# Layer 3's taps moved between TensorE and VectorE, and the next chunk's convolution and dt blocks paced over the scan steps

## The chip, the cores and the metric

The kernel runs on one core of one Trainium2 chip. The time is device time in microseconds of one launch. The engines are called as in the profile: PE is TensorE's matmul (PEld its weight load), DVE is VectorE, ACT is ScalarE, POOL is GpSimd, SP is SyncE, which here only issues DMAs.

## The reference, cut to what matters

Four residual layers on x of shape (8, 384, 32, 32), each after a group norm. Layers 0 and 2 hold a Mamba block over the 1024 positions of an image, layer 2 with a layer norm ahead and an MLP (384 to 1536 to 384) behind it. Layer 1 is a gated convolution with an 8x8 patch filter, layer 3 a depthwise 3x3 convolution.

```python
x = x + L0(_gn(x))      # Mamba
x = x + L1(_gn(x))      # 1x1, patch filter, depthwise 3x3, gate, 1x1
x = x + L2(_gn(x))      # layer norm, Mamba, MLP
x = x + L3(_gn(x))      # depthwise 3x3

# Mamba, per position l, channel d of 768, state n of 16
xm, z = split(x @ in_proj.T)
u  = silu(causal_conv3(xm) + conv_b)
dt, Bm, Cm = split(u @ x_proj.T)               # 24, 16, 16
dt = softplus(dt @ dt_proj.T + dt_b)
h  = exp(dt * A) * h + (dt * u) * Bm           # the scan over l
y  = (h . Cm + u * D) * silu(z)
out = y @ out_proj.T

# layer 3
conv_general_dilated(x, k, padding=1, feature_group_count=384)   # k: (384, 1, 3, 3)
```

## The kernel before, in words

**Tiling.** Each Mamba layer takes the 8 images as 16 chunks of T = 512 positions (two an image; chunk numbers n run from 0 to 15 for layer 0 and from 16 to 31 for layer 2, so that even n is an image's first half and odd n its second). The 768 x 16 states of a chunk are spread over 24 scan steps: a step holds 4 tiles of 128 partitions x 512 positions (8 channels x 16 states each). Steps are numbered through, 768 in all; `s["t"]` is the number of a chunk's first step (24 n). Six blocks of 128 channels (d = 0 to 5) make a chunk, and steps 4d to 4d+3 scan block d.

**One scan step** is made by nine generators (lines 745 to 900): `begins` loads g, the broadcast of dt*u, from DRAM up to five steps ahead (SP); `times` multiplies it by B (POOL, 128x2048); `decays` spreads dt by four matmuls into four PSUM tiles dA (PE); `exps` takes the exponent (ACT); `scans` runs four scans and two products with C (DVE); `states` does the other two products (POOL, 128x1024); `carries` saves the last column (ACT); `gathers` sums over states by matmuls into y (PE); `gatings` applies z (DVE).

**Work beside the scan.** While chunk n is scanned, the kernel prepares chunk n+1 and finishes earlier ones:
- `front` (line 594) of the next chunk: group norm (and layer norm), then six convolution blocks `block(d)` (line 619: three matmuls from in_proj, one ACT scale, two DVE multiply-adds; the function starts once chunk n-2's u buffers are free), SiLU, x_proj, and six dt blocks `step(d)` (line 668: one matmul, three ACT functions for softplus, a DVE add, the split of dt into three bf16 parts, one DMA `dtd`, and `scaled(d, v)`, line 718: dt*u on POOL and four DMAs `dud`). In layer 0 the split's first remainder is made by PE and the second by DVE; in layer 2 both are made by POOL.
- `gates` (line 548): the z projections and their SiLU. `finish` (line 905): the out-projection, which frees u, and in layer 2 the MLP (`mlp`, line 1152), one chunk after another.
- `layer1` (line 1020) and `layer3` (line 1215), once an image.

**Layer 3.** For each of three channel blocks k and two halves hf, `depthwise` (line 993) makes a diagonal 128x128 weight for each of the first `taps` taps (ACT) and multiplies it into one PSUM bank (PE); `take` (line 1242) then adds the other 9 - taps taps one after another by `scalar_tensor_tensor` on DVE, in the same bank, adds x and sends the result off. `TAPS, LAST_TAPS = 6, 4` (line 50): six taps on PE for images 0 to 6, four for image 7, whose layer 3 comes after the last scan. Layer 3 of image b runs for the most part from the middle of the next image's second chunk on.

**What sets the order.** `Order` (line 194 on) writes the program when the kernel is built: every piece of work is a generator that yields the engine it wants next and what must be ready; a clock model (`Clocks`) guesses when each engine is free, and of all that could begin, the earliest goes first. Each engine then runs its instructions in that fixed order and waits on semaphores. Nothing of the planner runs on the chip. Two helpers bear on the change:

```python
def pace(t):
    return once(lambda: ahead["scans"] >= 4 * min(t, len(steps)))
```

`pace(t)` holds a generator back until the planner has issued the scans of all steps before t; `together(due, gens)` starts several generators and waits for all. Three PSUM banks (`NBANK`) serve all products but dA and y; at most two dt blocks are between their matmul and their split at a time (`m_free`, `dt_free`, `pc_free`).

Of the kernel before, what the change touches and what calls it, by code (L numbers as in the profile page):

```python
# [17 lines left out]
B, C, H, W = 8, 384, 32, 32  # L18
# [8 lines left out]
NCH = L // T  # L27
# [19 lines left out]
NBANK = 3  # L47
LEAD = 2
PATIENCE = 6.0
TAPS, LAST_TAPS = 6, 4  # L50
SHARE = (2, 2, 2, 2)
SET_EXP = "natural_log_exp_and_others"

# [1 line left out]
def _flat(ap):  # L55
    return ap.rearrange("p a b -> p (a b)")


def _rows(ap):

    return ap.rearrange("(p k) l -> p k l", k=KC)
# [188 lines left out]
def tile_conv_preact_d4(ctx: ExitStack, tc: tile.TileContext, a: dict, out: bass.AP):  # L250
# [41 lines left out]
    def pace(t):  # L292

        return once(lambda: ahead["scans"] >= 4 * min(t, len(steps)))

    def once(test):
        return None, lambda: 0.0 if test() else None, None, False
# [38 lines left out]
    def product(name, pairs, when=None, read=()):  # L336

        ps = None
        for place, lhsT, rhs, start, stop in pairs:
            if ps is None:  # L340
                yield on("PE", rhs, lhsT, *read, when=both(bank, when) if when else bank)
                ps, tag = ps_take(name)
            else:
                yield on("PE", rhs, lhsT, next_=True)
            mm(place(ps), lhsT, rhs, start=start, stop=stop)
        return ps, tag
# [4 lines left out]
    def chain(name, terms, when=None, place=whole):  # L351
        terms = list(terms)
        last = len(terms) - 1
        return product(
            name,
            [(place, l, r, n == 0, n == last) for n, (l, r) in enumerate(terms)],
            when,
        )
# [172 lines left out]
    def projection(s, name, at):  # L531
        return chain(
            name, ((s["w"]["in"][:, k, at : at + P], s["xn"][:, k, :]) for k in range(KC))
        )
# [59 lines left out]
    def front(s):  # L594
        c, n, due = s["c"], s["n"], s["t"] - 26
        yield once(lambda: n == 0 or "normed" in chunks[n - 1] and (n == 1 or ("gates", 1) in chunks[n - 2]))
        yield on("SP")
        if n < NCH:
            xn = s["xn"] = first[n]
        else:  # L600
            xn = s["xn"] = new(wk, [P, KC, T], F32, "xf", 2)
            sync.dma_start(xn, _rows(s["src"][s["b"], :, c * T : (c + 1) * T]))
        if n % (B * NCH) == 0:
            yield from load_mamba(s["pre"])
        w = s["w"] = layer_w[s["pre"]]
        vec = w["vec"]
        yield once(lambda: "stats" in chunks[n - c])
        yield on("ACT", xn, chunks[n - c]["stats"][1])
        group_norm(_flat(xn), _flat(xn), chunks[n - c]["stats"])
        if s["pre"] == "l2_":  # L610
            yield from layer_norm(xn, due)
        s["normed"] = True
        yield once(lambda: n < 2 or "free" in chunks[n - 2])
        uh = s["u"] = [new(wk, [P, NH, T], F32, "u", 4) for _ in range(2)]
        u = [uh[d // NH][:, d % NH, :] for d in range(ND)]
        if c < NCH - 1:
            s["xt"] = new(wk, [P, ND, 2], F32, "xt")

        def block(d):
            ps, tag = yield from projection(s, "ps_in", d * P)  # L620
            yield on("ACT", ps)
            act(u[d], ps, AF.Identity, scale=vec[:, d, 2:3], bias=vec[:, d, 3:4])
            if c < NCH - 1:
                act(s["xt"][:, d, :], ps[:, T - 2 : T], AF.Copy)
            for j in (1, 2):
                yield on("DVE", u[d])
                vector.scalar_tensor_tensor(
                    u[d][:, j:T], ps[:, 0 : T - j], vec[:, d, 2 - j : 3 - j],
                    u[d][:, j:T], ALU.mult, ALU.add,
                )  # L630
            ps_give(ps, tag)

        yield from together(due, [block(d) for d in range(ND)])
        if c > 0:
            yield on("POOL", *u, due=-1)
            prev = chunks[n - 1]["xt"]
            hal = new(wk, [P, ND, 3], F32, "hal")
            gpsimd.tensor_mul(
                hal[:, :, 0:2], prev, vec[:, :, 0:1].to_broadcast([P, ND, 2])
            )  # L640
            gpsimd.tensor_mul(hal[:, :, 2:3], prev[:, :, 1:2], vec[:, :, 1:2])
            gpsimd.tensor_add(hal[:, :, 0:1], hal[:, :, 0:1], hal[:, :, 2:3])
            for h in range(2):
                gpsimd.tensor_add(
                    uh[h][:, :, 0:2], uh[h][:, :, 0:2], hal[:, h * NH : (h + 1) * NH, 0:2]
                )
        yield on("ACT", *u, when=session())
        for h in range(2):
            act(_flat(uh[h]), _flat(uh[h]), AF.Silu)
        exp_set()  # L650
        ps, tag = yield from chain(
            "ps_x", ((w["x"][:, d, :], u[d]) for d in range(ND)), place=lambda ps: ps[:RX, :]
        )
        yield once(lambda: n == 0 or "fronted" in chunks[n - 1])
        yield on("ACT", ps)
        dbc = new(wk, [RX, T], F32, "dbc")
        act(dbc, ps[:RX, :], AF.Identity, bias=one_row)
        ps_give(ps, tag)
        bc = s["bc"] = new(wk, [P, 2, T], F32, "bc", 2)
        s["dtd"], s["dud"], s["dts"] = {}, {}, {}  # L660

        def spread(j):
            ps, tag = yield from chain("ps_bc", [(selbc[:, j * P : (j + 1) * P], dbc)])
            yield on("ACT", ps)
            act(bc[:, j, :], ps, AF.Copy)
            ps_give(ps, tag)

        def step(d):
            ps, tag = yield from chain(
                "ps_dt", [(w["dt"][:, d * P : (d + 1) * P], dbc)],  # L670
                when=m_free.when,
            )
            m_free.take()
            m = new(wk, [P, T], F32, "spm", 2)
            yield on("ACT", ps)
            act(m, ps, AF.Abs)
            yield on("ACT", m)
            act(m, m, AF.Exp, scale=-1.0)
            yield on("ACT", m)
            act(m, m, AF.Ln, bias=1.0)  # L680
            yield on("DVE", m, when=dt_free.when)
            dt_free.take()
            v = new(wk, [P, T], F32, "dt", 2)
            vector.scalar_tensor_tensor(v, ps, 0.0, m, ALU.max, ALU.add)
            ps_give(ps, tag)
            yield on("ACT", v, when=pc_free.when)
            pc_free.take()
            pc = new(wk, [P, NPC, T], BF16, "pc", 2)
            act(pc[:, 0, :], v, AF.Copy)
            if s["pre"] == "l0_":  # L690
                yield on("PE", pc[:, 0, :], when=bank)
                rest, tag = ps_take("ps_dr")
                mm(rest, eye, v, stop=False)
                mm(rest, minus, pc[:, 0, :], start=False)
                m_free.give()
            else:
                yield on("POOL", pc[:, 0, :])
                gpsimd.tensor_sub(m, v, pc[:, 0, :])
                rest, tag = m, None
            order.add(scaled(d, v), s["t"] - 14)  # L700
            yield on("ACT", rest)
            act(pc[:, 1, :], rest, AF.Copy)
            if tag:
                yield on("DVE", pc[:, 1, :])
                vector.tensor_sub(pc[:, 2, :], rest, pc[:, 1, :])
                ps_give(rest, tag)
            else:
                yield on("POOL", pc[:, 1, :])
                gpsimd.tensor_sub(pc[:, 2, :], rest, pc[:, 1, :])
                m_free.give()  # L710
            yield on("SP", pc)
            to = dram.tile([NPC, P, T], BF16, tag="dtd", name="dtd", bufs=2 * ND)
            sync.dma_start(to.rearrange("p c t -> c p t"), pc)
            s["dtd"][d] = to
            pc_free.give()
            yield once(lambda: d in s["dud"])

        def scaled(d, v):
            yield on("POOL", u[d])
            gpsimd.tensor_mul(v, v, u[d])  # L720
            yield on("SP", v)
            to = dram.tile([E8 * NSUB, 4, T], F32, tag="dud", name="dud", bufs=2 * ND)
            for j in range(4):
                sync.dma_start(to[:, j, :], v[32 * j : 32 * (j + 1), :])
            s["dud"][d] = to
            dt_free.give()

        yield from together(due, [spread(j) for j in range(2)])
        yield from together(s["t"] - 14, [step(d) for d in range(ND)])
        s["fronted"] = True  # L730

# [733 lines left out]
```

## Time and profile before

| what | value |
|---|---|
| median of three runs | 6377.04 us (6371.48 to 6378.63) |
| the profiled execution | 6382.54 us, span 6380.8 us |
| first scan, last scan's end | 78.4 us, 6214.0 us |
| granted PE clock, mean | 0.964 |
| POOL, a step's two multiplies (128x2048, 128x1024) | 4537 ns + 2361 ns |
| DVE, a scan | 1205 to 1270 ns |
| DVE, a product with C | 675 ns |
| PE, matmul records of layer 3's depthwise | 552 |
| DVE, tap operations of layer 3 | 156 |

Busy time counts an engine's instructions as one union; the groups give the mean of one instruction and the idle time of its engine just before it, with what ended that. All engine calls go through one helper, so that all groups have its line, L189, and are told apart by their tiles. Tile names: `dA` decays, `g` the scanned input and result, `ps_in` convolution, `ps_dt`, `dt`, `spm`, `pc` the dt blocks, `ps_dw` from `xp` layer 3's depthwise (from `tp`: layer 1's), `ps_up`, `ps_dn`, `h` the MLP, `ps_out` the out-projection. A float32 matmul leaves two records.

### The profile page before, as it was taken

The numbers are of one execution on the slowest core, as the hardware profiler recorded it, in microseconds if no ns is written. First come the engines' busy times: TensorE is split into PE (matmuls) and PEld (weight loads), VectorE is DVE, ScalarE is ACT, GpSimd is POOL, SyncE is SP. The second block draws the span as 40 slices with busy tenths as digits, with TensorE's granted clock in tenths as the row PEclk, the third lists the DMA queues.
The fourth block names the chain that finished last, engine by engine and source line by source line (L and its number), as shares of the span: only waits on it lengthen the run. The fifth ranks groups of instructions, "written<-read, shape, count | busy, mean of one in ns | idle before, by whom it ended". The sixth has DMA issues, their size and how long they took to land.

```text
span 6380.8 us, 63205 instructions
## 1 busy us (share of the span) xinstructions
PE 5905.2 (93%) x19178; PEld 2228.3 (35%) x19178; DVE 5566.3 (87%) x6308; ACT 4268.3 (67%) x8024; POOL 5721.1 (90%) x2022
## 2 busy tenths in 40 slices
PE   6788999999999999989899999999999999999997
PEld 2223333333333333333333333333333333333333
DVE  4999989999999989988897898898988979989792
ACT  5666676767776666667766777667766667667652
POOL 4999999999999999989997998999989989989880
PEclk8789999999999999999999999999999999999998
DMA  6878778888877888877777787888778878878671
GB/s 167 196 190 199 176 192 191 200 198 210 188 188 189 190 190 189 199 187 185 181 181 194 196 207 184 192 209 200 197 178 196 204 185 197 186 197 202 173 177 37
DMA packets 345864, 1195.92 MB, mean 187 GB/s; under 512 B 40420, under 2 KB 142484, under 8 KB 247220
## 3 DMA queue, kind: packets, MB, share of 16 engines
q1 hardware_dynamic: 345524, 1191.88, 77.1%
q8 instruction: 154, 2.52, 0.2%
q14 instruction: 186, 1.52, 0.1%
HBM read 1040.73 MB, written 150.99 MB: 187 GB/s over the span
## 4 chain that ended last, share of the span: by engine, by line
DVE 30%; PE 27%; POOL 18%; ACT 10%; issue 9%; DMA 5%; SPq 0%; POOLq 0%; DVEq 0%; ACTq 0%
POOL g L189 17%; DVE g L189 14%; DVE dA L189 10%; PE ps_dw L189 5%; PE y L189 4%; DMA g<-dud 4%; PE ps_dn L189 3%; PE dA L189 3%; DVE u L189 3%; PE ps_up L189 3%; ACT dA L189 2%; PE ps_z L189 2%; PE ps_in L189 1%; ACT L370 1%; PE ps_t L189 1%
## 5 line engine op out<-in xcount | busy, mean ns | idle before, releaser
L189 POOL TENSOR_TENSOR g<-g,bc 128x1024 f32<-128x1024 f32 (+1 forms) x1536 | 5238.0, 3449 | 322.9 <-ACT carry L189 151.5
L189 ACT ACTIVATE dA<-dA,w_A 128x512 f32<-128x512 f32 x3072 | 2018.4, 661 | 1056.9 <-PE dA L189 1045.1
L189 PE MATMUL dA<-dts,selr 96*128 96x512 bf16 x3072 | 1192.9, 391 | 226.5 <-DVE g L189 207.5
L189 DVE TENSOR_TENSOR_SCAN g<-dA,carry,g 128x512 f32<-128x512 f32 x768 | 950.9, 1267 | 123.5 <-POOL g L189 108.0
L189 DVE TENSOR_TENSOR g<-dA,bc 128x512 f32<-128x512 f32 x1536 | 992.0, 675 | 24.3 <-ACT carry L189 23.3
L189 DVE TENSOR_TENSOR_SCAN g<-dA,g 128x512 f32<-128x512 f32 x768 | 903.3, 1205 | 111.2 <-POOL g L189 93.5
L189 DVE TENSOR_TENSOR_SCAN dA<-dA,carry,g 128x512 f32<-128x512 f32 x768 | 951.7, 1270 | 36.8 <-ACT dA L189 36.5
L189 DVE TENSOR_TENSOR_SCAN dA<-dA,g 128x512 f32<-128x512 f32 x768 | 907.0, 1210 | 62.6 <-ACT dA L189 62.4
L189 PE MATMUL y<-g,sely 128*32 128x512 f32 x6144 | 863.9, 631 | 64.8 <-POOL g L189 59.6
L189 PEld LDWEIGHTS <-selr 96*128 96x128 bf16 x3072 | 300.7, 99 | 1109.5 <-issue 1072.9
L189 PE MATMUL ps_dn<-h,mw 128*128 128x512 f32 x1152 | 563.4, 610 | 23.3 <-ACT h L189 11.8
L189 PE MATMUL ps_z<-xf,w_in 128*128 128x512 f32 x1152 | 567.5, 603 | 12.9 <-ACT z L189 5.2
L189 PE MATMUL ps_in<-xf,w_in 128*128 128x512 f32 x1152 | 551.1, 599 | 7.7 <-ACT xf L189 5.5
L189 PE MATMUL ps_up<-t,mw 128*128 128x512 f32 x1152 | 550.2, 596 | 7.1 <-ACT h L189 3.8
L189 PE MATMUL ps_out<-u,w_out 128*128 128x512 f32 x1152 | 551.6, 595 | 0.0
L189 PE MATMUL ps_dw<-tp,diag 128*128 128x512 f32 x864 | 436.5, 611 | 5.5 <-ACT diag L189 5.0
L189 PEld LDWEIGHTS y<-g,sely 128*32 128x32 f32 x6144 | 127.4, 109 | 628.5 <-POOL g L189 310.5
L189 PEld LDWEIGHTS ps_dn<-h,mw 128*128 128x128 f32 x1152 | 221.7, 196 | 290.5 <-issue 242.3
L189 PEld LDWEIGHTS ps_z<-xf,w_in 128*128 128x128 f32 x1152 | 218.0, 192 | 269.2 <-issue 213.7
L189 PEld LDWEIGHTS ps_in<-xf,w_in 128*128 128x128 f32 x1152 | 215.3, 191 | 275.5 <-issue 244.3
L189 PEld LDWEIGHTS ps_up<-t,mw 128*128 128x128 f32 x1152 | 214.6, 190 | 263.5 <-issue 228.2
L189 POOL TENSOR_TENSOR dt<-dt,u 128x512 f32<-128x512 f32 x192 | 243.2, 1277 | 70.5 <-ACT pc L189 61.3
(112 smaller groups left out, 6545.4 us busy)
## 6 DMA issues: line engine op xcount, KB each, us to landing
g<-dud SPq DMA_DIRECT2D x768, 1024.0 KB, 7.7
dtd<-pc SPq DMA_DIRECT2D x192, 384.0 KB, 4.0
dts<-dtd SPq DMA_DIRECT2D x192, 384.0 KB, 8.2
mw<-in_l_mlp_w SPq DMA_DIRECT2D x192, 384.0 KB, 6.4
dud<-dt SPq DMA_DIRECT2D x768, 64.0 KB, 3.0
xf<-in_x SPq DMA_DIRECT2D x16, 768.0 KB, 9.3
x<-in_x SPq DMA_DIRECT2D x16, 768.0 KB, 13.4
x_mid<-x SPq DMA_DIRECT2D x16, 768.0 KB, 5.1
```

What stands on the lines that cost most here:

```text
L189: return call(out_, *args, **kw)
L370: nc.scalar.preload_act_table_set(SET_EXP)
```

## The change

`TAPS` goes from 6 to 4, so that images 0 to 6 take four taps of layer 3 on PE and five on DVE, as image 7 did. In `front`, the convolution block d is not issued before step `s["t"] - 18 + d`, and the dt block d not before step `s["t"] - 9 + 3 * d`. Chunks 0, 15 and 16 are left as they were. Operations and buffers are otherwise the same.

```diff
-TAPS, LAST_TAPS = 6, 4
+TAPS, LAST_TAPS = 4, 4
...
         def block(d):
+            if n not in (0, B * NCH - 1, B * NCH):
+                yield pace(s["t"] - 18 + d)
             ps, tag = yield from projection(s, "ps_in", d * P)
             yield on("ACT", ps)
             act(u[d], ps, AF.Identity, scale=vec[:, d, 2:3], bias=vec[:, d, 3:4])
...
         def step(d):
+            if n not in (0, B * NCH - 1, B * NCH):
+                yield pace(s["t"] - 9 + 3 * d)
             ps, tag = yield from chain(
                 "ps_dt", [(w["dt"][:, d * P : (d + 1) * P], dbc)],
                 when=m_free.when,
```

## The prediction

> **What bounds the kernel now.** I read the page first (busy shares), then the groups by shape, then busy time by stretch, then the waits of the worst stretch.
>
> ```profile
> span 6380.8 us, 63205 instructions
> PE 5905.2 (93%) x19178; PEld 2228.3 (35%) x19178; DVE 5566.3 (87%) x6308; ACT 4268.3 (67%) x8024; POOL 5721.1 (90%) x2022
> ```
>
> Three engines are near full at once and ACT is not. An average does not say which one binds where, so I cut the trace at the start of each scan step (four DVE scans; 24 steps a chunk). First scan at 78 us, last scan's end at 6214 us. Chunks 2 to 14 (layer 0) take 179 us on average, chunks 18 to 29 (layer 2, with the MLP and layer 3 of earlier chunks) 201 us, and 167 us of tail follow. One image period of layer 2, from the answer for five stretches (columns: stretch, length, then busy us of PE, PEld, DVE, ACT, POOL; granted clock, DMA share, GB/s):
>
> ```profile
> 4931.62:5000.48 68.86, 60.32 (x179) 21.69 (x178) 64.08 (x76) 53.82 (x96) 64.06 (x32) 0.93 0.78 197
> 5000.48:5077.90 77.42, 75.97 (x247) 29.32 (x246) 70.36 (x80) 44.39 (x92) 67.15 (x20) 1.00 0.87 214
> 5077.90:5170.39 92.49, 89.53 (x302) 32.96 (x300) 88.45 (x100) 60.62 (x121) 92.33 (x33) 1.00 0.77 181
> 5170.39:5263.72 93.33, 88.80 (x252) 35.96 (x252) 53.13 (x59) 62.72 (x99) 65.31 (x33) 0.96 0.74 190
> 5263.72:5346.85 83.13, 81.80 (x272) 30.99 (x270) 81.55 (x92) 57.78 (x94) 78.65 (x24) 1.00 0.76 178
> ```
>
> These are **S1** odd chunk, steps 16 to 24 (five of the six layer-3 depthwise blocks start here); **S2** even chunk, steps 0 to 9; **S3** even, 9 to 22; **S4** even step 22 to odd step 5; **S5** odd, 5 to 16. Means of six such periods: S1 67.4 us (PE 62.0, DVE 63.6, POOL 65.1), S2 75.6 (73.7, 67.7, 66.3), S3 94.4 (91.6, 90.3, 93.9), S4 83.2 (78.8, 52.3, 63.9), S5 84.2 (82.6, 81.7, 80.3). S3 is POOL's (99%), S5 everybody's, S2 PE's. S4 is the loose one: seven steps in 83 us where seven at S3's pace (94.4/13) take 51, DVE idle for a third while PE is 95% busy. What it waits for:
>
> ```profile
> POOL spm L189 <- ACT pc L189: 19.3, 2, 10.0
> DVE x L189 <- PE ps_dn L189: 12.3, 3, 5.7
> DVE dt L189 <- ACT spm L189: 12.0, 2, 9.3
> DVE g L189 <- POOL g L189: 5.0, 2, 2.9
> ```
>
> The scans of the new odd chunk wait for its dt blocks, and those for a late front: its convolution starts 5 to 9 steps before the chunk in odd chunks (12 to 15 before even ones), because PE still has the MLP of older chunks to run.
>
> The groups that the change touches (busy us, mean ns, idle before):
>
> ```profile
> L189 PE MATMUL ps_dw<-xp,diag 128*128 128x512 f32 x552 | 280.1, 625 | 19.0 <-ACT diag L189 16.8 <-DVE dt L189 1.5 <-DVE acc L189 0.4
> L189 DVE SCALAR_TENSOR_TENSOR ps_dw<-xp,vec,ps_dw 128x512 f32<-128x512 f32 x156 | 115.2, 740 | 42.0 <-PE ps_dw L189 40.8
> L189 ACT ACTIVATE diag<-eye,vec 128x128 f32<-128x128 f32 x276 | 103.0, 405 | 47.7 <-PE ps_dw L189 46.8
> L189 POOL TENSOR_TENSOR dt<-dt,u 128x512 f32<-128x512 f32 x192 | 243.2, 1277 | 70.5 <-ACT pc L189 61.3
> L189 POOL TENSOR_TENSOR spm<-dt,pc 128x512 f32<-128x512 f32 x96 | 110.9, 1164 | 77.0 <-ACT pc L189 73.4 <-DMA g<-dud 3.4
> L189 POOL TENSOR_TENSOR pc<-spm,pc 128x512 bf16<-128x512 f32 x96 | 111.1, 1164 | 15.4 <-ACT pc L189 15.0
> ```
>
> A matmul's recorded duration is not its price, since records overlap:
>
> ```profile
> 4772.02 5.31 PE L189 MATMUL ps_z<-xf,w_in 128*128 128x512 f32 x12
> ```
>
> Twelve records in 5.31 us with a last one of 0.59 are 0.429 us apart. A float32 matmul has two records: **0.86 us each**.
>
> [...] I therefore price PE by starts. At 0.429 us a record a layer-2 chunk needs about 185 us, PE over 90% by that measure too. [...] the trace has 215 for the bf16 ones and twice that a record for float32. [...] The added DVE operation reads one tensor from PSUM and one from SBUF, and the 156 like it take 740 ns beside a POOL at 90%[...].
>
> **The change, part by part.**
>
> *Taps.* Images 0 to 6, six blocks each, two taps: 84. PE loses 84 x 0.86 = 72 us (10.3 an image). Upper end: the block's records start 0.50 us apart on average, waits for diagonals included, so up to 84 us. ACT loses 84 x 0.405 = 34 us: worth nothing where ACT is 64 to 79% busy (S1 to S5). DVE gains 84 x 0.74 = 62 us (8.9 an image). Image 7 already has four taps.
>
> *Convolution pacing* (block d not before step -18+d). Before, even layer-0 chunks start at -18 to -15, odd ones at -18 to -14, layer-2 chunks at -15 to -6. The pace holds back mostly even layer-0 chunks, by up to three steps, and their dt blocks then still begin near -9. I take 0: cover is the five or so steps until dt; were that gone, a boundary stall as in S4 would follow.
>
> *dt pacing* (block d not before step -9+3d: -9, -6, -3, 0, 3, 6). Before, six blocks come within some six steps ending near -2, in odd layer-2 chunks at -3 to +1. Block d is first used at step 4d, its load goes out up to five steps earlier: 4 to 5 steps of slack, no new stall. So blocks 3 to 5 move into the next chunk's steps 0 to 6. Each brings, in layer 2, POOL 1.28+1.16+1.16 = 3.6 us, PE 0.86, DVE 0.68, ACT about 3.1; in layer 0 POOL 1.28, DVE 1.35, PE 4 x 0.429 + 0.215 = 1.93; and on SP one dtd and four dud issues, about 2.1 us, in front of g loads that have four steps to spare.
>
> *Added waits.* The pace orders the program; no engine waits on it. The five chained DVE operations (3.7 us, were 2.2) hold a PSUM bank longer, while PE holds it 1.7 us less. Bounds -1 to +2 us an image; I take 0.
>
> *Layer 0* (means of six). Even 0 to 12: 101.9 us, PE 95.7; gets 5.8 of PE, I take half, +2.9. Even 12 to 24: 85.3, POOL 81.3; loses 3 x 1.28: -3.8. Odd 0 to 7: 49.4, PE 48.2; 5.8 less its 1.2 idle: +4.6. Odd 15 to 24: 64.3, POOL 64.3: -3.8. Sum -0.1 a pair: **0**, bounds +-4 on 6.5 pairs, +-26.
>
> *Layer 2, per image.* S1+S2 (143.0 us): DVE 131.3 + 8.9 = 140.2; at the 97% that DVE reaches in S5 that needs 144.5, at its present idle 11.7 it needs 151.9: +1.5 to +8.9, I take +2.5. POOL stays 131.4 over the two (10.8 moves from S1 to S2), PE falls by 10.3, which lets the MLP matmuls queued there go ahead. S3: POOL-bound, 0. S4: PE is 10.3 lighter before it, so MLP and out-projection end sooner, convolution and dt come sooner, and three dt blocks no longer crowd block 0; floor is POOL 63.9 + idle. I take -10 of a possible -19. S5: gets block 5, +1. Sum **-6.5**, six images: -39. Image 6 has its depthwise in chunk 31, where the last-but-one MLP runs until 6249 us, beyond the scans: -9 in the tail. Together **-48**. The profiled execution took 6382.5 (span 6380.8); -48 there is 6334, and from the median 6377.0 it is **6329**.
>
> **Rivals.**
> - *Larger gain, 6279.* S4 falls further towards its POOL floor: -14 an image, seven times, -98. For: S4's DVE is 31 of 83 us idle. Against: PE is 95% busy there and only 10 of that goes away.
> - *No change, 6377.* POOL binds S1, S3 and S5 (95 to 99%), and S4's gain is eaten by S1+S2. For: POOL's work is only moved.
> - *Slower, 6422: DVE becomes the bound in S1+S2.* Steps there stretch by the full 8.9 us an image (+62), the out-projection that frees the buffers of the odd chunk's convolution comes later with them, and S4 gives only the 2.4 from fewer dt blocks (-17): +45. For: DVE is 94% busy in S1. Against: it idles 7.9 us in S2. It decides once the stretch of S1+S2 exceeds what S4 gives back.
> - *The change does little of what it says*: true of convolution pacing, priced at 0 above.
>
> **How the numbers follow.** Forecast (6290 to 6363, 6329) 0.46; larger gain 0.17; no change 0.14; slower 0.23. A measurement here tells about 0.2% (13 us) from none. So faster 0.63, same 0.14, slower 0.23. Range 6262 to 6412: the larger gain reaches 6262 if S4 gives -16, and the top takes in most of the slower case; about 0.18 lies outside. The forecast's own range stands beside it, 6290 to 6363: layer 0's bounds and the S1+S2 bounds.
>
> **What would show it.** Right: x384 records of ps_dw from xp, 240 DVE operations at 740 ns, S1+S2 within 2% of 143 us, S4 near 73 with the odd convolution starting a step or more earlier, layer-0 chunks still near 179. Wrong: DVE over 97% in S1+S2 with that stretch above 150, S4 unchanged, or a new wait of POOL for g loads in steps 0 to 6.

## The result and the profile after

The changed kernel takes 6274.4 us (median of four runs, 6265.1 to 6281.3) against 6376.7 us for the kernel before beside it: ratio 0.984, 95% interval 0.9823 to 0.9857, that is 102 us less. The forecast was 48 us less. It had the direction right and the size wrong by more than a factor of two; the rival "larger gain" (6279 us) was the nearest.

The page of the changed kernel, its span and its busy shares:

```profile
span 6279.6 us, 62636 instructions
PE 5835.6 (93%) x19010; PEld 2196.0 (35%) x19010; DVE 5623.6 (90%) x6392; ACT 4234.9 (67%) x7940; POOL 5720.2 (91%) x2022
```

POOL's busy time is unchanged to 1 us (its work was only moved), DVE's rose by 57 us, PE's fell by 70. The touched groups of the changed kernel, busy us, mean ns, and idle before:

```profile
L189 PE MATMUL ps_dw<-xp,diag 128*128 128x512 f32 x384 | 196.1, 621 | 17.4 <-ACT diag L189 15.4 <-ACT h L189 1.2 <-DVE dt L189 0.5
L189 DVE SCALAR_TENSOR_TENSOR ps_dw<-xp,vec,ps_dw 128x512 f32<-128x512 f32 x240 | 176.7, 741 | 31.3 <-PE ps_dw L189 30.2
L189 ACT ACTIVATE diag<-eye,vec 128x128 f32<-128x128 f32 x192 | 69.2, 399 | 13.4 <-PE ps_dw L189 13.4
...
L189 POOL TENSOR_TENSOR spm<-dt,pc 128x512 f32<-128x512 f32 x96 | 111.1, 1161 | 33.2 <-ACT pc L189 31.1 <-ACT carry L189 2.0
```

Counts and durations are those forecast (384 records, 240 operations at 741 ns). POOL's wait for the dt blocks, in the last line, fell from 77 to 33 us.

The same five stretches of the same image period, S1 to S5, in the changed kernel (stretch, length, busy us of PE, PEld, DVE, ACT, POOL; clock, DMA share, GB/s):

```profile
4885.93:4961.87 75.94, 65.33 (x201) 24.60 (x200) 69.27 (x83) 46.36 (x73) 69.39 (x27) 0.93 0.71 182
4961.87:5038.30 76.43, 74.72 (x245) 28.49 (x244) 73.73 (x88) 55.43 (x110) 67.84 (x27) 1.00 0.85 221
5038.30:5131.49 93.19, 90.06 (x298) 34.09 (x298) 88.24 (x100) 68.73 (x133) 91.25 (x37) 1.00 0.79 189
5131.49:5194.13 62.64, 59.58 (x186) 22.28 (x185) 51.17 (x56) 45.68 (x77) 58.31 (x23) 0.97 0.82 207
5194.13:5280.03 85.90, 84.81 (x280) 32.43 (x279) 81.39 (x93) 54.68 (x84) 85.90 (x29) 1.00 0.83 196
```

The fourth line is where the time went: S4 was 93.33 us and is 62.64. Over the six periods:

| mean us of six | before | after | measured | forecast |
|---|---|---|---|---|
| S1 + S2 | 143.1 | 145.7 | +2.7 | +2.5 |
| S3 | 94.4 | 95.6 | +1.2 | 0 |
| S4 | 83.2 | 61.8 | -21.4 | -10 |
| S5 | 84.2 | 84.9 | +0.7 | +1 |
| image period | 404.9 | 388.0 | -16.9 | -6.5 |

Of the span's 101 us, chunks 18 to 29 gave 75, chunks 30 and 31 25, the tail 11; layer 0's chunks 2 to 14 lost 13, chunk 15 gave 16, chunks 16 and 17 lost 16, and the start gave some 3. What S4 waits for in the changed kernel (us in total, times, longest):

```profile
ACT h L189 <- PE ps_up L189: 4.8, 4, 2.2
DVE g L189 <- POOL g L189: 4.4, 3, 2.6
POOL spm L189 <- ACT pc L189: 4.0, 1, 4.0
...
DVE y L189 <- PE y L189: 3.2, 1, 3.2
```

POOL's 19.3 us of waiting for a late dt block have become 4.0, and DVE's 12.0 us for the same are no longer among the lines of that answer. In the six odd chunks the convolution now begins 11.5 to 13.9 steps ahead of the chunk (6.3 to 9.8 before) and the first dt block reaches DVE 3.7 to 6.3 steps ahead (0.7 to 2.8 before).

### The profile page after: what moved, and what is told of

It reads as the page before. It is cut to its first block, busy times and chain, and to the rows that moved or that the text cites. A ratio compares the mean times of both kernels' runs of the same rounds, so it can differ in the third digit from the quotient of the medians.

```text
span 6279.6 us, 62636 instructions
## 1 busy us (share of the span) xinstructions
PE 5835.6 (93%) x19010; PEld 2196.0 (35%) x19010; DVE 5623.6 (90%) x6392; ACT 4234.9 (67%) x7940; POOL 5720.2 (91%) x2022
## 4 chain that ended last, share of the span: by engine, by line
DVE 18%; PE 14%; POOL 12%; ACT 7%; issue 5%; DMA 3%; SPq 0%; DVEq 0%; POOLq 0%; ACTq 0%
POOL g L189 10%; DVE g L189 8%; DVE dA L189 5%; PE ps_up L189 3%; PE ps_dn L189 2%; PE y L189 2%; DMA g<-dud 2%; DVE ps_dw L189 2%; ACT dA L189 2%; PE dA L189 2%; DVE u L189 1%; PE ps_dw L189 1%; ACT h L189 1%; ACT L370 1%; ACT L189 1%
## 5 line engine op out<-in xcount | busy, mean ns | idle before, releaser
L189 DVE TENSOR_TENSOR_SCAN g<-dA,g 128x512 f32<-128x512 f32 x768 | 908.0, 1209 | 61.8 <-POOL g L189 43.9
L189 PE MATMUL ps_in<-xf,w_in 128*128 128x512 f32 x1152 | 574.0, 619 | 3.7 <-ACT xf L189 3.3
L189 PE MATMUL ps_dn<-h,mw 128*128 128x512 f32 x1152 | 556.5, 605 | 13.9 <-ACT h L189 8.0
```

Of the source, the lines that this page charges most:

```text
L189: return call(out_, *args, **kw)
```

## The experiments

The theories: **A**, PE's backlog makes the front of odd chunks late, so fewer taps alone shorten S4; **B**, the burst of dt blocks makes S4 long; **C**, only both help. After the first four runs came **D**: depthwise blocks and the dt burst of the next even chunk fall on the same steps, S1; and **E**: the burst that matters is the one in S4. All ratios are to the kernel before, run on the same chip, with 95% intervals.

**1. The taps alone.**

```diff
-TAPS, LAST_TAPS = 6, 4
+TAPS, LAST_TAPS = 4, 4
```

> Four taps on PE for images 0 to 6, no pacing. Theory A (PE's backlog makes the front of odd chunks late, so the stall S4 goes with PE's load): most of the change's 102 us, about 6300 us, S4 near 68 us. Theory B (the burst of six dt blocks at the boundary makes S4 long; the taps only load DVE): no gain or a loss, 6370 to 6420 us, S4 still about 80 us, S1+S2 longer by 5 to 9 us. Theory C (only both together help): 6350 to 6380 us.

Measured: 6378.5 us, ratio 1.0005 (0.9997 to 1.0014). Nothing. S4 did fall, to 76.2 us (-7.0), but S1+S2 rose to 150.0 (+7.0). Theory A falls; the total fits B and C alike, and S4 fits neither A nor B.

**2. Both paces, six taps.** The changed kernel with `TAPS, LAST_TAPS = 6, 4`.

> Six taps as before, both pacings. Theory A: little, 6350 to 6390 us, S4 near 78 us. Theory B: most of the 102 us, about 6290 us, S4 near 65 us. Theory C: 6350 to 6380 us. In all three, layer 0's chunks 2 to 14 take some 13 us more than before, as in the changed kernel, since the taps don't touch them.

Measured: 6348.8 us, ratio 0.9957 (0.9942 to 0.9972): -28 us. S1+S2 fell to 137.7 us (-5.3), S4 only to 81.9. Layer 0's chunks 2 to 14 took 2348 us (2332 before). With +2 for the taps and -28 for the paces, 76 of the 102 us belong to neither alone. Theory B is out (it had 6290 us); C holds, with the time 1 us below its range.

**3. dt pacing alone, six taps.** As 2, without

```diff
-            if n not in (0, B * NCH - 1, B * NCH):
-                yield pace(s["t"] - 18 + d)
```

> Six taps, dt blocks paced, convolution not. As with both pacings within 15 us if the convolution's pacing does nothing, which I priced at 0; layer 0's chunks 2 to 14 then also about 13 us over before.

Measured: 6353.5 us, ratio 0.9966 (0.9953 to 0.9978), 5 us from run 2: beside six taps the convolution's pacing does nothing measurable. Layer 0's chunks 2 to 14 took 2341 us.

**4. Four taps and dt pacing, no convolution pacing.** The edit of run 3, from the changed kernel.

> Four taps, dt blocks paced, convolution not. If the convolution's pacing is worth nothing: within 15 us of the changed kernel, 6260 to 6290 us.

Measured: 6314.7 us, ratio 0.9903 (0.9888 to 0.9918): 40 us over the changed kernel, a miss of my expectation. Five of its six S4 are 54 to 59 us (the changed kernel's are 54 to 73); one is 89, where the front of chunk 27 came late, as before the change.

**5. Four taps and convolution pacing, no dt pacing.** The changed kernel without

```diff
-            if n not in (0, B * NCH - 1, B * NCH):
-                yield pace(s["t"] - 9 + 3 * d)
```

> Four taps, convolution paced, dt blocks in bursts. Taps alone gave 6379 us, taps with dt pacing 6315, all three 6274. If the convolution's pacing is worth 40 us by itself where the taps are four, 6335 to 6345 us; if it helps only with dt pacing, or by the accident of another order, 6370 to 6390 us.

Measured: 6415.0 us, ratio 1.0058 (1.0043 to 1.0073), a loss outside what I expected. It lies in layer 0: its chunks 2 to 14 took 2369 us (2328 with the taps alone), of which chunk 15 gave 11 back. Chunks 18 to 29 took 2426.2 us, with the taps alone 2426.0, and from chunk 18 on DVE has the same operations in the same order in both kernels. So the convolution's pacing holds nothing back in layer 2 while the dt blocks come in bursts, and in layer 0 it is bad without dt pacing.

**6. Both paces in layer 2 alone, four taps.** In both conditions of the changed kernel:

```diff
-            if n not in (0, B * NCH - 1, B * NCH):
+            if n > B * NCH:
```

> The changed kernel with both pacings in layer 2 alone, layer 0 as before. Layer 0's chunks 2 to 14 took 13 us longer in the changed kernel, chunk 15 took 16 us less. If these cancel, 6270 to 6290 us; if the pacing in layer 0 is a pure loss there, 6260 us.

Measured: 6274.3 us, ratio 0.9839 (0.9822 to 0.9855), the time of the changed kernel. The gain is made in layer 2. It was not the gain of chunk 15 that cancelled layer 0's loss, though: chunks 16 and 17, which take 412 us in the changed kernel, take 396 here, as before the change, so that those 16 us are only handed on. In the traces layer 0's pacing is then a loss of some 13 us; the medians do not show it, and this stays open.

**7 and 8. dt pacing in even or odd chunks of layer 2 alone, four taps, no other pacing.** The convolution's two lines taken out, and

```diff
-            if n not in (0, B * NCH - 1, B * NCH):
+            if n > B * NCH and c == 0:
                 yield pace(s["t"] - 9 + 3 * d)
```

and in run 8 `c == 1`.

> Four taps; dt blocks paced in the even chunks of layer 2 alone, whose dt blocks fall among the depthwise blocks of S1; no other pacing. Theory D (the taps' gain is lost because the depthwise blocks and the dt burst crowd S1, where POOL and DVE are full and PE starves at 85%): S1 back from 76 to about 70 us with PE over 92%, S4 down to 60 to 66 us, 6300 to 6325 us in all. Theory E (the burst at the boundary S4 itself counts): no better than the taps alone, 6365 to 6385 us.

> Four taps; dt blocks paced in the odd chunks of layer 2 alone, at the boundary S4; no other pacing. Theory D: S1 stays at 74 to 77 us with PE near 85%, S4 at 70 to 76 us, 6355 to 6380 us in all. Theory E: S4 near 62 us, 6300 to 6325 us.

Measured: even chunks 6292.9 us, ratio 0.9868 (0.9853 to 0.9882); odd chunks 6346.5 us, ratio 0.9951 (0.9936 to 0.9966). Holding back the dt blocks of even chunks gives 84 of the 102 us. These blocks are issued in S1, in the steps of the depthwise blocks; S4 is where the odd ones are issued, and there it mattered less. Run 8 missed both theories: its 6346.5 us lie between E's range and D's, its S4 is 69.9 us, and in its S1 (73.7 us) PE is busy 88%. The six S1 of the taps alone (busy us in the order PE, PEld, DVE, ACT, POOL; the clock after them):

```profile
4118.28:4193.60 75.32, 63.08 (x187) 22.63 (x186) 70.09 (x84) 52.51 (x92) 70.43 (x33) 0.89 0.74 191
4522.68:4598.36 75.68, 63.11 (x185) 22.20 (x186) 70.21 (x84) 54.68 (x94) 73.44 (x34) 0.89 0.75 189
...
sum 456.30, PE 387.02 PEld 136.24 DVE 421.51 ACT 318.01 POOL 430.91; mean PE 64.50 PEld 22.71 DVE 70.25 ACT 53.00 POOL 71.82
```

and with the even chunks' dt blocks paced:

```profile
4111.37:4182.53 71.16, 69.67 (x220) 26.78 (x219) 68.82 (x83) 48.43 (x79) 64.18 (x26) 1.00 0.79 201
4499.68:4579.16 79.48, 74.97 (x227) 28.82 (x226) 69.62 (x83) 51.38 (x91) 62.01 (x26) 0.98 0.73 179
...
sum 438.25, PE 413.61 PEld 157.00 DVE 411.81 ACT 288.88 POOL 383.70; mean PE 68.93 PEld 26.17 DVE 68.64 ACT 48.15 POOL 63.95
```

Without pacing PE is busy 85% of S1 (387 of 456 us) and executes 191 records a stretch on average; with it 94% (414 of 438) and 213. POOL and DVE were the full ones (94% and 92%), and PE stood behind them. The longest wait of PE in one S1 of the taps alone (us in total, times, longest):

```profile
PE dA L189 <- DVE g L189: 6.8, 4, 2.8
```

Four decay matmuls waited there, 6.8 us together, for DVE to scan the tile that they overwrite: DVE was late with the scan. What PE's fixed order has behind such a matmul came after it, the MLP's matmuls among it; PE's own rows of the changed kernel show one such wait (start and length in us, in brackets the idle time and what ended it):

```profile
4945.96 1.02 PE L189 MATMUL ps_dn<-h,mw 128*128 128x512 f32 x2
4951.91 0.59 PE L189 MATMUL dA<-dts,selr 96*128 96x512 bf16 x1 [4.93 <-DVE g L189]
4952.29 4.03 PE L189 MATMUL ps_up<-t,mw 128*128 128x512 f32 x6
```

The wait of decay matmuls for DVE took 6.2 us an S1 with the taps alone, 2.5 before the change and 2.5 in run 7. A further 3.3 us (0.7 before, 0.2 in run 7) PE waited for DVE's `dt` and `acc` operations, the last ones on a PSUM bank; the prediction had put the longer holding of banks at 0. D holds for the larger part, E accounts for the smaller. D's number for S4 (60 to 66 us) was met, 64.9; S1 fell to 73.0, not to 70, and the total is better than I expected.

**9 and 10. DVE's price: two taps left out.** These two kernels compute layer 3 of images 0 to 6 without two of its nine taps: PE has four, DVE three as before.

```diff
-                    for t in range(taps, 9):
+                    for t in range(taps + 2 if b < B - 1 else taps, 9):
```

Run 9 is run 1 with this line, run 10 the changed kernel with it.

> No pacing, four taps on PE for images 0 to 6 and only three on DVE as before: two of the nine taps are left out there, so PE loses the work and DVE does not get it. If the added DVE operations are what starves PE in S1 beside the dt burst (6.2 us an S1 of PE's dA waiting for DVE in the taps-alone kernel, 2.5 before): S1 at most 68 us with PE over 90%, 6270 to 6310 us. If the burst alone spoils S1 as soon as PE is lighter: S1 over 72 us, 6340 to 6375 us.

> The changed kernel with the same two taps left out: the price that DVE pays in the changed kernel. If PE sets the period of layer 2 with pacing, DVE's 62 us are hidden: 6255 to 6276 us. If DVE now binds S1 and S2, 62 us come off in part: 6215 to 6250 us.

Measured: without pacing 6320.3 us, ratio 0.9908 (0.9894 to 0.9923); with pacing 6282.7 us, ratio 0.9852 (0.9836 to 0.9869). So the 84 DVE operations, 62 us of DVE work, cost 58 us without pacing (6378.5 - 6320.3) and in sum nothing with it (6274.4 - 6282.7 = -8): without them S1+S2 is 139.4 us instead of 145.7, but S4 is 67.1 instead of 61.8. Why S4 is longer there stays open. PE's relief (with ACT's diagonals, 34 us of an engine that is not full) is worth about the same either way: 60 us without pacing (0.9908), 66 with it (6348.8 - 6282.7). Run 9 is a little slower than I expected of its first case, and its S1 is 70.6 us with PE at 93%: so the burst seems to do some harm by itself.

**11. dt pacing in layer 2 alone, no convolution pacing, four taps.** Run 6 without the convolution's two lines.

> Four taps, dt pacing in layer 2 alone, no convolution pacing: against the kernel with both pacings in layer 2 alone (6274 us). If the convolution's pacing does nothing in layer 2, as the taps-and-convolution kernel had it (its layer 2 was that of the taps alone to 0.3 us): within 10 us, and the 40 us between the changed kernel and the one without convolution pacing come from another order of layer 0 and what follows. If it is needed: 6300 to 6315 us.

Measured: 6286.4 us, ratio 0.9858 (0.9843 to 0.9872), 12 us over run 6. Between the two cases, nearer to the first: most of the 40 us of run 4 has nothing to do with layer 2's convolution.

**12. Five taps.** The changed kernel with `TAPS, LAST_TAPS = 5, 4`.

> The changed kernel with five taps on PE. Six gave 6349 us, four 6274 us. If each tap moved saves PE the same (PE sets the period): half way, 6305 to 6318 us. If the gain comes with a threshold (the front of odd chunks in time or not): near one of the two ends.

Measured: 6306.4 us, ratio 0.9891 (0.9876 to 0.9906): -42 us for the first tap moved, -32 for the second. This is near enough to half way and speaks for a rate rather than a threshold.

**13 and 14. Three and two taps.** The changed kernel with 3 and with 2.

> The changed kernel with three taps on PE for images 0 to 6: PE loses another 42 matmuls (36 to 43 us), DVE gains another 31 us. If DVE still has room: 6235 to 6250 us. If DVE is at its edge in S1, S2 and S5 (95 to 97% busy in the changed kernel): 6265 to 6300 us.

> Two taps on PE. With room on DVE: 6200 to 6230 us; at the edge: DVE's 62 us more than in the changed kernel outweigh PE's, 6290 to 6350 us.

Measured: 6282.8 us, ratio 0.9846 (0.9829 to 0.9862), and 6315.2 us, ratio 0.9905 (0.989 to 0.992). Four is at the edge: three taps gain nothing (8 us more, less than the scatter that run 15 shows), two lose 41 us. With three, S4 seems to have nothing left to give; four of its six S4 stretches:

```profile
3959.41:4013.35 53.94, 53.32 (x174) 20.13 (x173) 48.03 (x52) 36.03 (x58) 53.94 (x21) 1.00 0.92 210
4349.06:4402.09 53.03, 52.13 (x172) 19.84 (x171) 48.04 (x52) 36.29 (x59) 53.03 (x21) 1.00 0.93 226
4741.34:4795.62 54.28, 52.88 (x175) 20.20 (x174) 48.51 (x53) 37.18 (x60) 54.28 (x21) 1.00 0.92 223
5132.03:5186.62 54.59, 53.67 (x177) 20.61 (x176) 48.69 (x53) 38.40 (x64) 53.20 (x22) 1.00 0.95 232
```

POOL, the last of the five busy times, fills three of these four stretches, and PE is busy 98% of the time: some 54 us is the floor for seven steps with what is left of the dt blocks in them. S1+S2 meanwhile grew to 153.4 us.

**15. The dt pacing one step later.**

```diff
-                yield pace(s["t"] - 9 + 3 * d)
+                yield pace(s["t"] - 8 + 3 * d)
```

> The changed kernel with each dt block held one step longer. No work is added or removed, and block 0 still has three steps before its first use: within 10 us of 6274 if the order is robust; 6290 to 6320 us if small shifts of the order are worth as much as the convolution's pacing seemed to be.

Measured: 6299.6 us, ratio 0.9875 (0.9858 to 0.9891): 25 us for a shift that adds and removes no work. Differences of this size between two kernels of this study can be the order that the planner happened to find; the 12 us of run 11 lie in that scatter, the 40 of run 4 are more than it, and what the convolution's pacing adds beside dt pacing stays open. The gain itself is not such scatter: the six kernels with four taps and dt pacing at least in layer 2's even chunks (the changed one and runs 4, 6, 7, 11 and 15) take 6274 to 6315 us, each at least 63 us less than the taps alone.

No version beat the changed kernel; run 6 equals it.

## Why the prediction came out too small

*What bounds the kernel* held: S4 was the loose stretch, and its cause was the late front. Over 36 boundaries into odd chunks, in the kernels of before, after and runs 1 to 4, S4 takes 60 us on average where the convolution began at least 11 steps ahead (12 cases), 77 at 9 to 11 steps (9), 84 at less than 9 (15).

*The taps*: PE's price (72 us, upper end 84) measured 60 and 66; DVE's durations were exact. The sum for S1+S2 came out in the changed kernel (+2.5 forecast, +2.7 measured), but in part by luck: by run 10 DVE's operations alone lengthen it by 6.3 us.

*The step that failed* is "S4: ... I take -10 of a possible -19", through the worth given to dt pacing; S4 gave -21.4. I capped S4's gain by the work that leaves PE, 10.3 us an image, and added nothing for the pacing (the "slower" rival has 2.4 us an image for it). In S1 I counted the three blocks that move away as POOL's work, moved from S1 to S2 with "POOL stays 131.4", and as nothing more. Runs 7, 8, 9 and 10 show what they are worth: their going lets PE run in S1, where it then does 68.1 us of work in 71.9 us instead of 62.0 in 67.4, although 5.7 us of taps have left it (30.3 depthwise records a stretch instead of 43.7, 0.43 us each). With four taps in both kernels it is 68.9 us in 73.0 (run 7) against 64.5 in 76.0 (run 1). The MLP's matmuls take the room. Their records (`ps_up` and `ps_dn`), mean of six:

| stretch | before | taps alone (run 1) | even dt blocks paced (run 7) | changed |
|---|---|---|---|---|
| S1 | 43.0 | 51.8 | 82.8 | 80.0 |
| S4 | 95.7 | 85.2 | 85.3 | 72.5 |

So MLP matmuls that stood in S4's way are done three stretches earlier, the front of the odd chunk comes four steps sooner, not "a step or more", and S4's PE time falls by 18 us instead of 10. The floor "POOL 63.9 + idle" had the same fault: it left in S4 the dt blocks that the pacing takes out. POOL's time there fell to 57.4 us, and S4, at 61.8, ends below that floor.

In terms of the sum: the forecast of -48 us had -69 for PE (-10 in S4 for six images and -9 in the tail), +15 for DVE and +6 for the dt blocks in S5. Measured were -60 to -66 for PE; -28 (run 2) to -38 (run 10 against run 9) for the paces, for which the forecast had no gain of their own; and nothing for DVE's work where the dt blocks are paced. PE's term was right as a whole, the other two were mis-sized.

*Rivals.* "Larger gain" named the right place, S4 falling towards POOL's floor, and run 13 shows that floor. Its counter-argument, that only 10 us of PE work goes away there, was the error. "DVE becomes the bound in S1+S2" is what the taps alone do: +7.0 us there, of the 8.9 priced; it was a fair price for the kernel without pacing, where it ate S4's gain of 7.0. I had treated the two edits as a sum; they are not one. "No change" failed because S1+S2 gave back only 2.7 of S4's 21.4 us.

*Layer 0 at 0* held for its 16 chunks (-5 us), by +13 in chunks 2 to 14 and -16 in chunk 15, but chunks 16 and 17 then took 16 us more. Both were outside my working. The traces of the kernels with dt pacing in layer 0 have 403 to 415 us for chunks 16 and 17, those without pacing there 394 to 399. *Convolution pacing at 0*: held in layer 2 beside bursts (0.2 us of 2426) and beside six taps (5 us); it costs 41 us in layer 0's chunks 2 to 14 where the dt blocks are not paced. The reason for that was not tried.

*The tail* gave 11 us where I had 9.

*Readings that were off* without changing the argument: nearer four than five of the six depthwise blocks start in S1; 0.50 us is the busy time of a depthwise record, while the records of a block start 0.65 us apart on average, other work between them; and -16 us an image for S4 makes 6265 us, not 6262.

## What to carry to other kernels

In this kernel, with PE 93%, POOL 90 to 91% and DVE 87 to 90% busy before and after the change, an operation had no fixed price: the same 62 us of DVE work cost 58 us in one order and nothing in another. Before pricing a move from engine to engine, list what else is issued in the very steps where the moved work lands, and ask which full engine the lightened one waits for; a change that spreads the other work may be what makes the move pay. And where a queue carries a backlog, look for the cause of a stall earlier: with the taps alone PE was starved in S1 (85% busy), and the stall showed three stretches later, in S4 (76.2 us, against 61.8 in the changed kernel).

## What the runs showed of the hardware

A starved PE was also a slower PE here. In S1 of the taps-alone kernel, with PE busy 85%, the granted clock averaged 0.90 (0.83 in the worst stretch); it was 0.97 before and 0.98 in the changed kernel and in run 7, where PE was busy 94 to 95%. The traces of the kernels before and after record the clock as full or half, in stretches that are multiples of 3.41 us, the last of each trace excepted. At half clock, two records of a 128x512 float32 matmul of the projections or the MLP start 0.853 us apart, at full clock 0.429 (medians of 35 and 4101 pairs in the trace of before).

What goes ahead of a change of the clock was counted in windows of 3.41 us, from the first scan to the last, in these two traces. A window at full clock in which PE was busy under 40%, as the profile records it, was followed by one at half clock in all 54 cases, at 40 to 70% in 63 of 158, and above 70% in none of 3124. From half clock it came back after 112 of 120 windows busy 90% or more, and after none of 71 under 80%. So half clock also followed windows in which PE was idle only in part. How much of the lost time is the clock and how much the waiting was not separated.

DVE's operation with one PSUM and one SBUF input kept its price at both loads: 740 ns at 156 operations and 741 at 240, with POOL 90 and 91% busy beside it.
